# Two attention steps to a turn, query tiles in halves, and an adjacency that is transposed before it is scaled

## The chip, the cores and the metric

The kernel runs on one core of a Trainium2 chip. The metric is the device time of one execution in microseconds (us), as the median of some runs. Every run counted here was in the fast state (its granted clock and its time agree with the fastest of the same kernel), so fast runs are compared with fast runs. A profile names the engines PE (TensorE), PEld (its weight loads), DVE (VectorE), ACT (ScalarE), POOL (GpSimd) and SP. L473 is line 473 of that kernel's source. The changed kernel's lines stand 15 or 16 higher in the attention part than the same lines before.

## The reference

Sixteen batches of 1024 nodes with 256 features. Layer 0 aggregates with a normalized adjacency and runs two linear layers with batch norms; layer 1 is graph-weighted attention with four heads of 64. Each layer is followed by a residual and a layer norm.

```python
# layer 0
A_norm = A + jnp.eye(n)
deg = jnp.sum(A_norm, axis=0) + jnp.sum(A_norm, axis=1) - jnp.diagonal(A_norm)
dinv = jax.lax.rsqrt(deg)
A_hat = A_norm * dinv[:, None] * dinv[None, :]
agg = jnp.einsum('nm,bmd->bnd', A_hat, features)
# ... relu(batchnorm(agg @ W1.T + b1)), then batchnorm(h @ W2.T + b2)
# layer 1 (cut): Wg = adj * a symmetric gate from the column means of x
g = jax.nn.relu(jnp.einsum('bcn,bnm->bcm', fea, Wg) * para)      # the queries
k, v = ...                                                       # x @ kv_w
attn = jax.nn.softmax(jnp.einsum('bhnd,bhmd->bhnm', q, k) * scale, axis=-1)
out = jnp.einsum('bhnm,bhmd->bhnd', attn, v)
```

## The kernel before

The preamble sums the columns of A with one-column matmuls (`pd`), scales the rows of A, transposes A (`pat`) and scales again while the transposes are evicted.

```python
pd = ps.tile([P, FB], F32, tag="a", name="pd")
for j in range(NT):
    for i in range(NT):
        nc.tensor.matmul(pd[:, j : j + 1], A[i][:, ts(j, P)], ones, start=(i == 0), stop=(i == NT - 1))
# ... deg, dinv, A[i] scaled by dinv on VectorE, then transposes (pat) evicted with the second scale
```

Attention runs in 16 steps a batch. A step is one scores product `s` (with its exponentials on ACT), one product `o` of exponentials and values, and between them "fillers": work that prepares the next batch or finishes the last one. All fillers share three PSUM banks, the pool `ps_t`.

```python
ps_s = pool("ps_s", 2, space=PSUM)      # scores, two tiles of two banks
ps_o = pool("ps_o", 1, space=PSUM)
ps_t = pool("ps_t", 3, space=PSUM)      # every filler: pf, px, py, pg, pk, pv, pc, pd

def x1_t(b, j):                          # filler: px, evicted by ACT
    p = ps_t.tile([P, FB], F32, tag="t", name="px")
    for c in range(CT):
        nc.tensor.transpose(p[:, ts(c, P)], x1s[b, j][:, ts(c, P)], ident)
    nc.scalar.copy(x1Ts[b][:, :, ts(j, P)], p[:, :C].rearrange("p (c n) -> p c n", c=CT))

def finish_a(b, i):                      # filler: pf, read by two VectorE instructions
    p = ps_t.tile([P, FB], F32, tag="t", name="pf")
    # ... three transposes into p
    nc.vector.reciprocal(rd, p[...])
    nc.vector.tensor_mul(r, p[...], rd)  # cut: views and broadcast; p is free after this
    nc.vector.tensor_add(r, r, x1s.pop((b, i)))
    # ... statistics of r, nm on GpSimd

for g in range(...):                     # the plan: at[g] holds the fillers of step g
    scores(g + 1); exps(g + 1); sums(g)
    for f, a in at.get(g, []):
        f(*a)
    attend(g)
```

The other fillers are `ln1_a` (py, read by VectorE), `graph` (pg, eight 512-column matmuls into one bank), `keys` (pk), `values` (pv), `crow` (pc, row sums `cs` made into a row) and `dens` (pd, denominators).

Of the kernel before, what the change touches and what calls it, by code (L numbers as in the profile page):

```python
# [9 lines left out]
F32 = mybir.dt.float32  # L10
AF = mybir.ActivationFunctionType
OP = mybir.AluOpType
AX = mybir.AxisListType
# [3 lines left out]
P = 128  # L17
# [5 lines left out]
def gnn_norm_attention_kernel(  # L23
# [16 lines left out]
    nc = tc.nc  # L40
    B, N, C = x.shape
# [4 lines left out]
    FB = 512  # L46
# [31 lines left out]
    yT_all = dram.tile([B, P, CT, N], F32, name="yT")  # L78
    yT_dram = [yT_all[b] for b in range(B)]

    LDP = 3
    s2 = const.tile([P, CT], F32, name="s2")
    t2 = const.tile([P, CT], F32, name="t2")

# [1 line left out]
    with ExitStack() as l0:  # L86
# [29 lines left out]
        with ExitStack() as ph1:  # L116
# [21 lines left out]
            w2n = xp.tile([P, CT, H], F32, tag="w2n", bufs=1, name="w2n")  # L138
            nc.sync.dma_start(w2n, W2.rearrange("(c p) d -> p c d", p=P))
            load_x(0)  # L140
            b1t, g1t, be1t = (load_vec(v, HT, n) for v, n in ((b1, "b1t"), (g1, "g1t"), (be1, "be1t")))
            b2t, g2t, be2t = (load_vec(v, CT, n) for v, n in ((b2, "b2t"), (g2, "g2t"), (be2, "be2t")))
            load_x(1)

            deg = w0.tile([P, NT], F32, name="deg")
            diag = w0.tile([P, NT], F32, name="diag")
            scr = w0.tile([P, P], F32, name="scr")
            for i in range(NT):
                blk = A[i][:, ts(i, P)]
                nc.vector.tensor_add(blk, blk, ident)  # L150
                nc.vector.tensor_reduce(deg[:, i : i + 1], A[i], AX.X, OP.add)
                nc.vector.scalar_tensor_tensor(
                    scr, blk, 1.0, ident, op0=OP.mult, op1=OP.mult, accum_out=diag[:, i : i + 1]
                )

            for c in range(HT):
                p = ps.tile([P, FB], F32, tag="a", name="pw1")
# [6 lines left out]
                    nc.tensor.transpose(p[:, ts(k, P)], w2n[:, c, ts(k, P)], ident)  # L164
                nc.scalar.copy(W2T[:, :, ts(c, P)], p.rearrange("p (k f) -> p k f", k=HT))

            pd = ps.tile([P, FB], F32, tag="a", name="pd")
            for j in range(NT):
                for i in range(NT):
                    nc.tensor.matmul(  # L170
                        pd[:, j : j + 1], A[i][:, ts(j, P)], ones, start=(i == 0), stop=(i == NT - 1)
                    )
            nc.vector.tensor_add(deg, deg, pd[:, :NT])
            nc.vector.tensor_sub(deg, deg, diag)
            dinv = w0.tile([P, NT], F32, name="dinv")
            rsqrt(dinv, deg, 0.0)

            AhT = ahp.tile([P, NT, N], F32, name="AhT")
            for i in range(NT):
                nc.vector.tensor_scalar_mul(A[i], A[i], dinv[:, i : i + 1])  # L180
            for j in range(NT):
                for h in range(NH):
                    p = ps.tile([P, FB], F32, tag="a", name="pat")
                    for k in range(FB // P):
                        i = h * (FB // P) + k
                        nc.tensor.transpose(p[:, ts(k, P)], A[i][:, ts(j, P)], ident)
                    if h % 2:
                        nc.vector.tensor_scalar_mul(AhT[:, j, ts(h, FB)], p, dinv[:, j : j + 1])
                    else:
                        nc.scalar.mul(AhT[:, j, ts(h, FB)], p, dinv[:, j : j + 1])  # L190


            def aggregate(b):
                aggT.append(aggp.tile([P, CT, N], F32, tag="agg", name=f"agg{b}"))
                for c in range(CT):
                    for h in range(NH):
                        p = ps.tile([P, FB], F32, tag="a", name="pa")
                        for k in range(NT):
                            nc.tensor.matmul(  # L199
                                p,  # L200
                                xts[b][:, k, ts(c, P)],
                                AhT[:, k, ts(h, FB)],
                                start=(k == 0),
                                stop=(k == NT - 1),
                            )
                        nc.scalar.copy(aggT[b][:, c, ts(h, FB)], p)  # L206
                load_x(b + 2)
# [113 lines left out]

    def ln_stats(sm, r, name):

        st = sm.tile([P, 6], F32, tag="st", name=f"st_{name}")
        nc.vector.bn_stats(st, r)
        mv = sm.tile([P, 2], F32, tag="mv", name=f"mv_{name}")
        nc.vector.bn_aggr(mv, st)  # L327
        rs = sm.tile([P, 1], F32, tag="rs", name=f"rs_{name}")
        rsqrt(rs, mv[:, 1:2], EPS)
        return mv, rs  # L330
# [4 lines left out]
    def fast():  # L335
      with ExitStack() as fx:
        pool = lambda name, bufs, **k: fx.enter_context(tc.tile_pool(name=name, bufs=bufs, **k))
        x1p = pool("x1p", 21)
        x1Tp = pool("x1Tp", 1)
        crp = pool("crp", 1)  # L340
        wgp = pool("wgp", NT)
        kp = pool("kp", 2 * CT)
        qp = pool("qp", CT + 1)
        vp = pool("vp", 2)
        ep = pool("ep", 5)
        accp = pool("accp", 3)
        otp = pool("otp", 3)
        sm = pool("sm", 6)
        rp = pool("rp", 4)
# [13 lines left out]

        def begin(b):
            x1Ts[b] = x1Tp.tile([P, CT, N], F32, tag="x1T", name=f"x1T_{b}")
            css[b] = sm.tile([P, NT], F32, tag="cs", name=f"cs_{b}")

        def ln1_a(b, j):
            p = ps_t.tile([P, FB], F32, tag="t", name="py")
# [25 lines left out]
        def crow(b):  # L395

            nc.vector.tensor_scalar_mul(css[b], css[b], 1.0 / C)
            hcs[b] = sm.tile([P, NT], F32, tag="hcs", name=f"hcs_{b}")
            nc.vector.tensor_scalar_mul(hcs[b], css[b], 0.5)
            crows[b] = crp.tile([P, N], F32, tag="crow", name=f"crow_{b}")  # L400
            for h in range(NH):
                p = ps_t.tile([P, FB], F32, tag="t", name="pc")
                for k in range(FB // P):
                    j = h * (FB // P) + k
                    nc.tensor.transpose(p[:, ts(k, P)], css[b][:, j : j + 1].to_broadcast([P, P]), ident)  # L405
                nc.scalar.copy(crows[b][:, ts(h, FB)], p)
# [44 lines left out]
        def graph(b, m):  # L451

            h, c, k = m // (CT * NT), m // NT % CT, m % NT
            if k == 0:
                pg[b] = ps_t.tile([P, FB], F32, tag="t", name="pg")
                if h == 0:
                    qTs[b, c] = qp.tile([P, N], F32, tag="qT", name=f"qT_{b}_{c}")
            nc.tensor.matmul(  # L458
                pg[b], x1s[b, k][:, ts(c, P)], wgs[b, k][:, ts(h, FB)], start=(k == 0), stop=(k == NT - 1)
            )  # L460
            if k == NT - 1:
                qs = qTs[b, c][:, ts(h, FB)]
                nc.vector.tensor_mul(qs, pg[b], para_sb[:, c, ts(h, FB)])
                nc.vector.tensor_scalar(qs, qs, 0.0, scale, op0=OP.max, op1=OP.mult)

# [6 lines left out]
        def scores(g):  # L472
            b, hf, pair, cp = step(g)  # L473
            for a in range(2):
                cb = 2 * cp + a
                t = ps_s.tile([P, 2, FB], F32, tag="s", name=f"s{g}_{a}")
                for h in range(2):
                    nc.tensor.matmul(  # L478
                        t[:, h, :],
                        kTs[b, pair][h * HD : (h + 1) * HD, ts(cb, P)],  # L480
                        qTs[b, pair][h * HD : (h + 1) * HD, ts(hf, FB)],
                        start=True,
                        stop=True,
                    )
# [99 lines left out]
            nc.vector.tensor_add(badi[0], bad[:, 0:1], bad[:, 1:2])  # L584


        NS = NT // 2 * NP * NH
        at = {}

        def put(w, s, f, *a):  # L590
            at.setdefault(w * NS + s, []).append((f, a))

        for b in range(B):

            put(b - 2, 4, begin, b)
            for j in range(NT):
                if b > 0 or j >= LDP:
                    put(b - 2, 3 + j, load, b, j)
                put(b - 2, 4 + j, bn2, b, j)
                put(b - 2, 5 + j, ln1_a, b, j)  # L600
                put(b - 2, 7 + j, ln1_b, b, j)
                put(b - 2, 8 + j, x1_t, b, j)
            put(b - 2, 7 + NT, crow, b)
            for i in range(NT):
                put(b - 2, 8 + NT + i, wg_a, b, i)
                put(b - 2, 8 + NT + i, wg_b, b, i)

            n = 0
            kv = [(keys, (b, c, h)) for c in range(CT) for h in range(NH)]
            kv += [(values, (b, j)) for j in range(0, NT, 2)]  # L610
            for n, (f, a) in enumerate(kv):
                put(b - 1, n * 5 // len(kv), f, *a)
            ng = CT * NH * NT
            for m in range(ng):
                put(b - 1, 6 + m * 10 // ng, graph, b, m)

            for i in range(NT):
                hf = i // (FB // P)
                s = (hf + 1) * (NS // NH)
                if i % (FB // P) == 0:  # L620
                    put(b, s, dens, b, hf)
                put(b, s + 1 + i % (FB // P), finish_a, b, i)
                put(b, s + 2 + i % (FB // P) + (b == B - 1 and hf == NH - 1), finish_b, b, i)
        put(B - 1, NS // NH, range_so_far)
        put(B - 1, NS + FB // P, range_all)

        nsteps = B * NS
        for g in range(min(at), max(max(at), nsteps - 1) + 1):
            if 0 <= g + 1 < nsteps:
                scores(g + 1)  # L630
                exps(g + 1)
            if 0 <= g < nsteps:
                sums(g)
            for f, a in at.get(g, []):
                f(*a)
            if 0 <= g < nsteps:
                attend(g)
        return nc.values_load(
            badi[0][0:1, 0:1],
            min_val=0,  # L640
# [156 lines left out]
```

## Time and profile before

| | us |
|---|---|
| time, median of 3 runs | 2816.97 |
| first aggregation matmul (pa) | 62.4 |
| first scores | 1012.0 |
| from one batch's first scores to the next, 13 times | 114.92 |
| last scores end to the end of the span | 20.6 |

The prediction shows the page and the chain. One more view is needed here: what TensorE waited for in one steady batch (the one after seven others). The columns are engine, tile and line that waited, what released it, us in total, times, and the longest.

```profile
PE pc L405 <- DVE cs L397: 1.2, 1, 1.2
```

That is the whole answer: in 114.92 us TensorE waits once. Whatever makes a batch shorter must shorten TensorE's own stream.

### The profile page before, as it was taken

How to read it: one execution, taken by the hardware profiler on the slowest of the kernel's cores; microseconds unless marked ns; L12 is line 12 of the kernel's file. 1: busy time of each engine (PE TensorE's matmuls, PEld its weight loads, DVE VectorE, ACT ScalarE, POOL GpSimd, SP SyncE). 2: the span in 40 equal slices, each digit the busy share in tenths (PEclk: the TensorE clock that was granted, in tenths of full speed). 3: DMA queues.
4: the chain of work that ended last, by engine and by line, in shares of the span. 5: the costliest groups of instructions: out<-in, count | busy, mean ns of one | idle time of the engine just before them, and what ended most of it. 6: DMA issues, size and time to landing. Idle time of an engine off the chain costs nothing.

```text
span 2816.4 us, 26243 instructions
## 1 busy us (share of the span) xinstructions
PE 2750.9 (98%) x9426; PEld 1174.2 (42%) x9426; DVE 1352.6 (48%) x2364; ACT 1295.2 (46%) x1871; POOL 498.2 (18%) x660
## 2 busy tenths in 40 slices
PE   7999999999999899999999999999999999999998
PEld 6444444444444443434434434344343443434432
DVE  3011110111312456657666576575766756657556
ACT  1111111111555654646646556465564664655634
POOL 0000000000000113223122231232322313223113
PEclk9999999999999899999999999999999999999999
DMA  3121221130384200101001010010100100101000
GB/s 105 60 75 60 90 84 65 76 119 0 134 306 142 81 29 27 34 12 43 25 23 34 16 41 27 19 40 16 36 30 16 42 23 27 34 14 42 10 8 24
DMA packets 109993, 147.02 MB, mean 52 GB/s; under 512 B 10272, under 2 KB 92704, under 8 KB 103712
## 3 DMA queue, kind: packets, MB, share of 16 engines
q1 hardware_dynamic: 109856, 145.27, 15.0%
q8 instruction: 77, 1.26, 0.2%
q14 instruction: 60, 0.49, 0.1%
HBM read 86.52 MB, written 58.72 MB: 52 GB/s over the span
## 4 chain that ended last, share of the span: by engine, by line
PE 96%; DVE 2%; DMA 0%; ACT 0%; issue 0%; POOL 0%; SPq 0%; DVEq 0%; POOLq 0%; ACTq 0%
PE s L478 17%; PE o L508 17%; PE pg L458 16%; PE pa L199 16%; PE po L288 8%; PE ph L212 8%; PE pk L431 4%; PE pv L442 4%; PE pf L538 2%; PE pd L527 1%; PE py L371 1%; PE pd L170 1%; PE px L392 1%; PE pc L405 1%; PE pf L539 0%; DMA w1n<-in_L_gnn_W_dram 0%
## 5 line engine op out<-in xcount | busy, mean ns | idle before, releaser
L490 ACT ACTIVATE e<-s 128x1024 f32<-128x1024 f32 x512 | 496.4, 1022 | 409.2 <-PE s L478 408.7
L478 PE MATMUL s<-qT,kT 64*128 64x512 f32 x2048 | 508.8, 615 | 0.0
L508 PE MATMUL o<-e,v 128*64 128x512 f32 x2048 | 495.7, 605 | 0.0
L499 DVE TENSOR_TENSOR acc<-acc,e 128x1024 f32<-128x1024 f32 x384 | 466.9, 1216 | 41.5 <-ACT e L490 27.5
L458 PE MATMUL pg<-wg,x 128*128 128x512 f32 x1024 | 475.4, 602 | 1.5 <-DVE wg L423 1.3
L199 PE MATMUL pa<-AhT,x 128*128 128x512 f32 x1024 | 441.9, 592 | 0.0
L231 DVE BATCH_NORM_STATS2 st<-ph 128x6 f32<-128x512 f32 x128 | 89.4, 698 | 567.3 <-ACT hT L230 567.3
L478 PEld LDWEIGHTS s<-qT,kT 64*128 64x128 f32 x2048 | 176.2, 186 | 327.0 <-issue 244.8
L199 PEld LDWEIGHTS pa<-AhT,x 128*128 128x128 f32 x1024 | 194.5, 190 | 244.4 <-issue 244.2
L458 PEld LDWEIGHTS pg<-wg,x 128*128 128x128 f32 x1024 | 181.6, 190 | 240.5 <-issue 213.0
L423 DVE SCALAR_TENSOR_TENSOR wg<-wg,adj_sb 128x1024 f32<-128x1024 f32 x128 | 156.8, 1225 | 171.7 <-ACT wg L419 169.5
L206 ACT COPY agg<-pa 128x512 f32<-128x512 f32 x64 | 37.5, 586 | 402.3 <-PE pa L199 402.3
L212 PE MATMUL ph<-agg,W1T 128*128 128x512 f32 x512 | 222.2, 592 | 0.0
L508 PEld LDWEIGHTS o<-e,v 128*64 128x64 f32 x2048 | 124.2, 136 | 225.5 <-issue 212.6
L66 POOL TENSOR_SCALAR rs_z<-mv_z 128x1 f32<-128x1 f32 x128 | 52.2, 408 | 900.3 <-DVE mv_z L327 884.4
L66 POOL TENSOR_SCALAR rs_a<-mv_a 128x1 f32<-128x1 f32 x128 | 124.8, 975 | 435.8 <-DVE mv_a L327 435.7
L288 PE MATMUL po<-hL,W2T 128*128 128x512 f32 x384 | 165.0, 592 | 0.0
L68 POOL TENSOR_TENSOR rs_a<-rs_a,mhalf 128x1 f32<-128x1 f32 x128 | 157.9, 1234 | 10.7
L66 POOL TENSOR_SCALAR rs_bn<-mv_bn 128x1 f32<-128x1 f32 x6 | 1.3, 222 | 894.7 <-DVE mv_bn L104 894.7
L393 ACT COPY x1T<-px 128x256 f32<-128x256 f32 x128 | 47.7, 372 | 239.9 <-PE px L392 239.9
L212 PEld LDWEIGHTS ph<-agg,W1T 128*128 128x128 f32 x512 | 97.3, 190 | 122.5 <-issue 122.2
L230 ACT COPY hT<-ph 128x512 f32<-128x512 f32 x128 | 75.0, 586 | 144.7 <-PE ph L212 144.7
(101 smaller groups left out, 2540.7 us busy)
## 6 DMA issues: line engine op xcount, KB each, us to landing
h<-hT SPq DMA_DIRECT2D x24, 1024.0 KB, 3.8
hL<-h SPq DMA_DIRECT2D x24, 1024.0 KB, 6.4
x<-in_x_dram SPq DMA_DIRECT2D x16, 1024.0 KB, 5.4
yT<-y SPq DMA_DIRECT2D x32, 512.0 KB, 3.6
yt<-yT SPq DMA_DIRECT2D x128, 128.0 KB, 2.5
xr<-in_x_dram SPq DMA_DIRECT2D x128, 128.0 KB, 2.3
out_dram<-r SPq DMA_DIRECT2D x128, 128.0 KB, 1.7
A<-in_adj_dram SPq DMA_DIRECT2D x4, 1024.0 KB, 8.3
```

The lines of the kernel that those rows point to most:

```text
L66: nc.gpsimd.tensor_scalar(dst, src, add, None, op0=OP.add)
L68: nc.gpsimd.tensor_tensor(dst, src, mhalf[:, :n], OP.pow)
L199: nc.tensor.matmul(p, xts[b][:, k, ts(c, P)], AhT[:, k, ts(h, FB)], start=(k == 0), stop=(k == NT - 1),)
L212: nc.tensor.matmul(p, W1T[:, k, ts(f, P)], aggT[b][:, k, ts(h, FB)], start=(k == 0), stop=(k == CT - 1),)
L288: nc.tensor.matmul(po[c], W2T[:, k, ts(c, P)], hT[u][:, k, :], start=(k == 0), stop=(k == HT - 1))
L423: nc.vector.scalar_tensor_tensor(t, t, 1.0, adj_sb[:, i, :], op0=OP.add, op1=OP.mult)
L431: nc.tensor.matmul(p, kvw[:, k, ts(c, P)], x1Ts[b][:, k, ts(h, FB)], start=(k == 0), stop=(k == CT - 1))
L458: nc.tensor.matmul(pg[b], x1s[b, k][:, ts(c, P)], wgs[b, k][:, ts(h, FB)], start=(k == 0), stop=(k == NT - 1))
L478: nc.tensor.matmul(t[:, h, :], kTs[b, pair][h * HD : (h + 1) * HD, ts(cb, P)], qTs[b, pair][h * HD : (h + 1) * HD, ts(hf, FB)], start=True ...
L490: nc.scalar.activation(E[g, a], S.pop((g, a)), AF.Exp)
L499: nc.vector.tensor_add(ACC[b, hf, pair], ACC[b, hf, pair], E[g, a])
L508: nc.tensor.matmul(O[b, hf, pair][h * HD : (h + 1) * HD, :], vs[b][:, cb, pair * P + h * HD : pair * P + (h + 1) * HD], E[g, a][:, h, :], ...
```

## The change

The intent is to save two things: the column-sum matmuls ahead of the first useful work, and the changes of tile shape on TensorE. Two steps now make a turn, with one run of fillers in it, and every filler gets a new place in one of eight turns a batch. The query tiles are cut into halves so that they can be freed sooner. The pools are resized to match (E 5 to 6, acc 3 to 2, x1 21 to 22). `ps_t` keeps its three banks.

```diff
 preamble (cut)
-            pd = ps.tile([P, FB], F32, tag="a", name="pd")
-            ... NT * NT one-column matmuls, A scaled, transposes evicted with a scale
+            for h in range(NH):
+                ...
+                        nc.tensor.transpose(p[:, ts(k, P)], A[i][:, ts(j, P)], ident)   # raw A
+                    ... evicted with accum_out=col[:, h, j : j + 1], on VectorE or ACT
+            ... deg and dinv, then both scales in one VectorE instruction a row block
 plan (cut)
+        WG = (3, 3, 1, 1)
+        KV = (3, 3, 2)
+        QG = (6, 6, 6, 7, 7)
+                put(b - 2, j // 2 + 2, ln1_a, b, j)        # two py in a turn
+                put(b - 2, j // 2 + 4, x1_t, b, j)         # two px in a turn
+                    put(b, t + 1 + k // 2, finish_a, ...)  # two pf in a turn
+            put(b - 2, NC - 1, crow, b)
 loop (cut)
-        for g in ...: scores(g + 1); exps(g + 1); sums(g); fillers; attend(g)
+        rank = {dens: 0, finish_a: 1, finish_b: 2, x1_t: 3, ln1_a: 4, ln1_b: 5}
+        for t in ...:
+            g = 2 * t
+            now = sorted(at.get(t, []), key=lambda fa: rank.get(fa[0], 9))
+            scores(g + 2); exps(g + 2); dens of now; sums(g)
+            the other fillers of now; sums(g + 1)
+            scores(g + 3); exps(g + 3)
+            attend(g); attend(g + 1)
```

Note the sort: in each turn all pf come first, then px, then py, and only then the long products pg, pk and pv.

> **What bounds the kernel now.** I read the page's engine shares, then the chain that ended last, then the timeline of TensorE and of the engines it works with, in three stretches.
>
> ```profile
> span 2816.4 us, 26243 instructions
> PE 2750.9 (98%) x9426; PEld 1174.2 (42%) x9426; DVE 1352.6 (48%) x2364; ACT 1295.2 (46%) x1871; POOL 498.2 (18%) x660
> ...
> PE 96%; DVE 2%; DMA 0%; ACT 0%; issue 0%; POOL 0%; SPq 0%; DVEq 0%; POOLq 0%; ACTq 0%
> ```
>
> TensorE (PE) carries 96% of the chain; VectorE (DVE) and ScalarE (ACT) have half their time free. A change helps only where it shortens TensorE's own stream or removes its waits. The long pieces of the chain of waits, in order of time, show the preamble:
>
> ```profile
> 3.01 12.11 DMA w1n<-in_L_gnn_W_dram
> 18.90 27.11 PE pd L170 x128
> 48.18 5.40 DVE A L180 x8
> 53.63 8.90 PE pat L186 x57
> 62.53 54.94 PE pa L199 x128
> ```
>
> Useful matmuls start at 62.4 us. Before them stand 27 us of one-column matmuls (column sums of A), a rescaling, the transposes. After that the chain has 429 ns per matmul instruction (54.94/128), the full rate for 512 columns. Marks by stage, from first starts of groups in the timeline: aggregation 62.4, second linear layer 723, its end 945, first scores 1012.0, last scores end 2795.8. In attention a batch of 16 steps takes 114.92 us, the same thirteen times over. One step on TensorE (start, length):
>
> ```profile
> 1656.34 2.74 PE L458 MATMUL pg<-wg,x 128*128 128x512 f32 x6
> 1658.91 0.38 PE L392 MATMUL px<-ident,x 128*128 128x128 f32 x2
> 1659.13 0.38 PE L371 MATMUL py<-ident,yt 128*128 128x128 f32 x2
> 1659.44 1.94 PE L508 MATMUL o<-e,v 128*64 128x512 f32 x8
> 1661.31 1.99 PE L478 MATMUL s<-qT,kT 64*128 64x512 f32 x8
> 1663.23 0.44 PE L538 MATMUL pf<-ident,ot 128*128 128x128 f32 x2
> ```
>
> Eight instructions of o or s run as four pairs, so 4 x 0.429 = 1.72 us at full rate; from start to start o takes 1.87 and s 1.92. From raw starts: leaving any group for one of another tile shape costs 0.09 us, and the second start in the new shape comes 0.10 late (s, pg, pk) or 0.05 late (o, transposes). So TensorE never waits here, except once per batch (1.2 us, pc for DVE's cs), but pays about 0.5 us per step in three shape switches. And the chain that frees a pf buffer, on VectorE:
>
> ```profile
> 1656.54 0.18 DVE L541 RECIPROCAL RD<-pf 128x4 f32<-128x4 f32 x1 [0.72 <-PE pf L539]
> 1656.75 0.42 DVE L543 TENSOR_TENSOR r<-pf,RD 128x256 f32<-128x256 f32 x1
> 1657.21 0.43 DVE L548 TENSOR_TENSOR r<-r,x 128x256 f32<-128x256 f32 x1
> 1657.67 0.43 DVE L325 BATCH_NORM_STATS2 st_z<-r 128x6 f32<-128x256 f32 x1
> 1658.13 0.18 DVE L327 BATCH_NORM_AGGREGATE mv_z<-st_z 128x2 f32<-128x6 f32 x1
> 1658.23 0.45 DVE L379 SCALAR_TENSOR_TENSOR x<-x,mv_a,rs_a 128x256 f32<-128x256 f32 x1
> ```
>
> The pf buffer is free when L543 ends, 0.9 us after the last pf transpose starts; a second finish behind it on VectorE begins 1.69 us later. Today one pf stands in a step and nothing needs its buffer soon.
>
> **What the Trainium skill says.** "TensorEngine Tiling (Array Packing)", Key Properties: changing the tiling mode drains TensorE. The trace agrees: the 0.14 to 0.20 us per switch above. "PSUM — Partial Sum Buffer" gives 8 banks of 2 KiB per partition: scores (2 x 2 banks), o (1) and the ps_t pool (3) use all, so ps_t can't grow. "Trainium Kernel Development and Optimization", Best Practices: consistent bubbles can mean that PSUM ran out; the kernel before shows none, and I expect them now. "TensorE: Matmul & The Clock Gate", Part 1: the clock is halved until TensorE has been busy for a window. The trace agrees: transposes start every 213 ns until 58.7 us and every 109 after.
>
> **The change, part by part.**
>
> *Preamble.* A is transposed raw, column sums come from accumulating evictions, and both scales are applied afterwards, so the 27 us of pd go, and the transposes no longer wait for them. New path: A lands from 5.7 us (first VectorE work) to about 13 (4 MB at the 415 GB/s of that window). 32 cold transposes x 0.213 = 6.8 us per half. VectorE is slower: per half four diagonals (0.29 + 0.36), two row sums of 1.22 and four evictions of about 0.8, some 8.5 us with waits; both halves end near 24.7. Degree sums 0.6, the power on POOL 1.7 (L68 dinv took 1.66), four cold transposes 0.9, first scaling 0.75: pa starts at 29. Scaling one row block (0.7) is faster than its two matmuls (0.86), so it stays ahead. Cold clock for the first matmuls: 1 to 3 us lost. Net -31 us.
>
> *Shape switches.* A turn is s, fillers, s, o, o instead of twice s, fillers, o. The second o follows the first without a switch: -0.15 us per turn, 1.2 per batch. There are 8 runs of fillers per batch instead of 16, each 0.15 to 0.20 for entering and leaving: -1.4. Scores still enter twice. Sum -2.6 us per batch. Scores, o and filler matmuls themselves are the same number.
>
> *Buffers.* The plan now puts two finishes, two px and two py in one turn, all transposes first. In the new program's order and its waits, with three ps_t banks (often one held by pg), I find for a steady batch, turns 0 to 7, time from the start of the turn's first scores (1.92 long; exps done at 3.1, as the exponentials of the step above start 1.17 after their scores and take 1.94; pf at 1.92 and 2.31, its reciprocal 0.59 later as above; a px copy on ACT starts 0.42 after px, as 1658.91 to 1659.33 shows, and takes 0.37):
> - Turn 5: px waits for the first pf's buffer (L543 ends 3.15); the second px for ACT's copy of the first (4.07); py for the next copy (4.9); the second py for the second pf's buffer, free at 4.84 (2.51 + 1.69 + 0.64). pg resumes at 5.36 instead of 3.51: 1.85 us lost.
> - Turn 6: px at 3.2, its copy is behind two 0.6 us finish activations on ACT (exps till 3.1, so copied at 4.75); pg at 5.0 instead of 3.1: 1.9.
> - Turn 4: px and py wait for the dt copy and px copies: pg at 4.84 instead of 3.85: 1.0.
> - Turn 2: pv waits for the second pf's buffer, 4.9 instead of 3.08: 1.8.
> - Turn 7: pc directly follows pg rather than px, so its wait for cs (qT 0.69 + 0.43, cs 0.17) grows by 0.2.
> - Turns 0, 1, 3: pk or pg separate the reuses; ACT (11 to 13 us of work in turns of 13.5) and VectorE (at most 13.2) keep up; no loss.
> Sum +6.75. Query halves only free qT earlier (5 half buffers are enough); nobody waited for qT, so worth 0.
>
> Net per steady batch -2.6 + 6.75 = +4.2 us. Fourteen windows have the full plan, the first without turn 2: 14 x 4.2 - 1.8 = +57. The next to last has no px or py and gains 2.4, the last gains 1. Start-up: without attention to cover it, ACT's wg before the kT copies and pairs of layer norms cost a little, +2 to the first scores. At the end four o groups instead of two follow the last scores: +3.6.
>
> Sum: -31 + 57 - 3.4 + 2 + 3.6 = +28, so 2845 us.
>
> **Rivals.**
> *(a) The waits don't happen* or hide: then -2.6 x 16 - 31 + 3 = -70, about 2748, faster by 2.5%. For it: VectorE and ACT average half idle, and every engine passes its per-turn sum. Against: the waits stand in the program, matmuls run in order, and each latency is one that the trace shows at its shortest, with the waiting engine idle.
> *(b) More waits than counted*: VectorE in turns 1 and 2 (13.2 of 13.5 us, then both finishes) falls behind, so finishes begin late, or exps(g+3), behind all ACT fillers and needing E buffers that only o(g) frees, delays the next scores. Each 1 us per turn in two turns is 28 us: near 2875, slower by 2%. For it: the sums on VectorE come last in the turn; against: two attends (3.6 us) of slack.
> *(c) The preamble alone matters*: if attention comes out even, about 2790. That needs the losses to halve.
>
> **Range and chances.** The preamble is uncertain by 4 us, start-up and end by 4, switches (s to o has no record yet) by 6, the buffer waits by 1 us per batch, or 14. Together 18 for one deviation; with (a) and (b) as tails: 2810 to 2875. Faster by over 2% (under 2760.6) needs (a): 0.08. Slower by over 2% (over 2873.3): 0.12. Within: 0.80.
>
> **What would show it.** First pa at 29 to 32 us instead of 62.4. In attention, a period near 119 us per batch; idle before px, py, pg and pv on TensorE, released by L543's successor on VectorE and by ACT's x1T copies, about 6.5 us per batch, in four of eight turns; TensorE busy near 94% in attention. o's second group starts 0.43 us after the last pair of the first, not 0.52. Wrong if the period is under 115 (waits hidden), if scores themselves wait for exps (then (b)), or if pa starts after 36 us.

## The result, and the profile after

The changed kernel is correct and takes 2846.47 us (median of 4 runs, 2846.23 to 2846.97), against 2816.83 for the kernel before in the same rounds. The ratio is 1.0106, 95% interval 1.0089 to 1.0124: the same within 2%, and 1% slower. Ratios here and below are the mean time of one kernel's fast runs over the mean of the other's fast runs of the same rounds, so they are not quite the ratios of the medians quoted.

The page of the changed kernel:

```profile
span 2844.6 us, 26117 instructions
...
PE 2713.6 (95%) x9306; PEld 1157.5 (41%) x9306; DVE 1349.9 (47%) x2377; ACT 1289.3 (45%) x1887; POOL 321.0 (11%) x660
```

TensorE was busy for 2750.9 us of 2816.4 before and is for 2713.6 of 2844.6 now: it works 37 us less and stands idle 65 us more. (The page's chain of waits was followed back only over the last few us of this kernel, so it says nothing here.)

The preamble is in TensorE's timeline (start, length, line, tile, and in brackets the idle time before it and what ended that):

```profile
9.65 6.58 PE L170 MATMUL pat<-ident,A 128*128 128x128 f32 x50
...
23.32 1.09 PE L188 MATMUL pdr<-ident,dinv 128*128 128x128 f32 x8 [1.85 <-POOL dinv L68]
24.95 5.37 PE L215 MATMUL pa<-AhT,x 128*128 128x512 f32 x8 [0.54 <-issue]
```

The aggregation starts at 24.95 instead of 62.37. The first eight matmuls take 5.37 us where full speed takes 3.4, as the clock is halved from 25.2 to 28.7. The first scores come at 976.51 instead of 1012.04, so 35.5 us earlier.

Attention gives all of it back. The period is 119.19 us instead of 114.92. These are TensorE's waits in one steady batch, the whole answer, in the columns of the one line before:

```profile
PE pc L421 <- DVE cs L413: 1.4, 1, 1.4
PE pv L458 <- DVE r L558: 1.4, 1, 1.4
PE px L408 <- ACT x1T L409: 1.2, 2, 0.7
PE px L408 <- DVE r L558: 1.0, 2, 0.5
PE py L387 <- ACT x1T L409: 0.7, 2, 0.5
PE px L408 <- ACT dt L544: 0.4, 1, 0.4
PE py L387 <- PE py L387: 0.2, 1, 0.2
```

Every tile that waits is a filler, and every releaser (`r L558`, `x1T`, `dt`) but two is the instruction that reads another filler's bank last. The two are `cs`, which pc needs as data, and py itself. Turn 5 of this batch shows how, first on TensorE:

```profile
1893.96 0.38 PE L553 MATMUL pf<-ident,ot 128*128 128x128 f32 x2
1894.18 0.27 PE L554 MATMUL pf<-ident,dt 128*128 128x128 f32 x1
1894.95 0.41 PE L408 MATMUL px<-ident,x 128*128 128x128 f32 x2 [0.50 <-DVE r L558]
1895.83 0.44 PE L408 MATMUL px<-ident,x 128*128 128x128 f32 x2 [0.46 <-ACT x1T L409]
1896.72 0.66 PE L387 MATMUL py<-ident,yt 128*128 128x128 f32 x4 [0.46 <-ACT x1T L409]
```

then on VectorE and on ACT at the same time:

```profile
1894.38 0.42 DVE L558 TENSOR_TENSOR r<-pf,RD 128x256 f32<-128x256 f32 x1
...
1896.04 0.42 DVE L558 TENSOR_TENSOR r<-pf,RD 128x256 f32<-128x256 f32 x1
```

```profile
1895.40 0.37 ACT L409 COPY x1T<-px 128x256 f32<-128x256 f32 x1 [0.62 <-PE px L408]
1896.30 0.37 ACT L409 COPY x1T<-px 128x256 f32<-128x256 f32 x1 [0.53 <-PE px L408]
```

The turn starts at 1891.66. The first px starts when the first pf's product ends (1894.38 + 0.42 = 1894.80), the second px when the copy of the first has ended (1895.77), py when the next copy has (1896.67). ACT waited for px and TensorE for ACT: both were idle by turns, TensorE for about 0.5 us at each hand-over. Before, a step held at most one pf, one px and one py: in the prediction's excerpt six 512-column products stand between pf and px, px and py follow each other without a wait, and the next px comes a step later.

I measured the waits turn by turn from TensorE's start-to-start times, counting what exceeds the interval of an undisturbed pair (109 ns for a transpose, 216 for pv, 429 for the 512-column products). This counts from start to start, so it comes out a little larger than the idle times of the view above.

| turn | length before | length after | of it waits | where |
|---|---|---|---|---|
| 7 | 17.45 | 16.50 | 1.58 | pc |
| 0, 1, 3 | 42.17 | 40.32 | 0 | |
| 2 | 11.79 | 14.15 | 1.93 | second py, pv |
| 4 | 14.55 | 15.64 | 0.88 | second px, second py |
| 5 | 15.41 | 16.31 | 1.92 | px, second px, py |
| 6 | 13.55 | 16.28 | 1.53 | px, second px |

Fillers moved between turns, so single lengths before and after do not compare; their sums do (114.92 and 119.20), and the waits of a turn do with its own order. In the kernel before the only entry is 1.36 for pc.

One thing had not been foreseen. Two of the thirteen steady periods are 120.88 and 120.86 us long, and the record of the clock shows it halved for 3.4 us in turn 5 of each. These are stretches of the changed kernel with the busy time of each engine (TensorE's first) and the granted clock as the third value from the end. The first two rows are such a place, the last two the same place one batch earlier:

```profile
1653.40:1656.80 3.40, 1.98 (x13) 1.19 (x12) 2.50 (x8) 2.05 (x4) 0.75 (x2) 1.00 0.00 0
1656.80:1660.20 3.40, 3.40 (x8) 1.84 (x8) 3.19 (x12) 0.00 (x0) 2.45 (x9) 0.50 0.03 5
1534.20:1537.60 3.40, 1.98 (x13) 1.18 (x12) 2.49 (x8) 2.06 (x4) 0.75 (x2) 1.00 0.00 0
1537.60:1541.00 3.40, 3.40 (x12) 1.73 (x13) 3.19 (x12) 0.00 (x0) 2.44 (x9) 1.00 0.00 0
```

Both stretches hold the same matmuls and the same three waits, yet only one was followed by half clock, at a cost of 1.7 us. All changes of the clock in this trace lie on multiples of 3.4133 us from each other (the two halvings are 210 multiples apart). On that grid the first stretch fills one window, and the one a batch earlier lies across two, as the period of 119.19 is 34.92 windows and the waits slide over the grid. That this decides when the clock is halved is likely, but not shown. How long TensorE was busy in a window does not decide it by itself: the two windows before the halvings hold 1.99 us of work, but seven windows in turn 2 of the same trace hold 1.81 us (1731.91 to 1735.32 is one), and none of them was followed by half clock.

### The profile page after: what moved, and what is told of

Same layout as the page of the kernel before. It is cut to its first block, busy times and chain, and to the rows that moved or that the text cites. A ratio compares the mean times of both kernels' runs of the same rounds, so it can differ in the third digit from the quotient of the medians.

```text
span 2844.6 us, 26117 instructions
## 1 busy us (share of the span) xinstructions
PE 2713.6 (95%) x9306; PEld 1157.5 (41%) x9306; DVE 1349.9 (47%) x2377; ACT 1289.3 (45%) x1887; POOL 321.0 (11%) x660
## 5 line engine op out<-in xcount | busy, mean ns | idle before, releaser
L523 PE MATMUL o<-e,v 128*64 128x512 f32 x2048 | 467.7, 598 | 0.0
L473 PE MATMUL pg<-wg,x 128*128 128x512 f32 x1024 | 455.6, 595 | 0.0
L473 PEld LDWEIGHTS pg<-wg,x 128*128 128x128 f32 x1024 | 189.5, 191 | 210.6 <-issue 203.9
L523 PEld LDWEIGHTS o<-e,v 128*64 128x64 f32 x2048 | 135.6, 136 | 316.4 <-issue 315.6
L511 DVE TENSOR_TENSOR acc<-e,e 128x1024 f32<-128x1024 f32 x64 | 78.2, 1222 | 206.1 <-PE pd L542 206.1
L439 DVE SCALAR_TENSOR_TENSOR wg<-wg,adj_sb 128x1024 f32<-128x1024 f32 x128 | 155.2, 1221 | 38.6 <-ACT wg L435 35.1
L66 POOL TENSOR_SCALAR rs_z<-mv_z 128x1 f32<-128x1 f32 x128 | 37.5, 293 | 1197.7 <-DVE RD L556 1168.6
L478 DVE TENSOR_TENSOR qT<-pg,para_sb 128x512 f32<-128x512 f32 x64 | 44.2, 690 | 199.2 <-PE pg L473 198.9
L458 PE MATMUL pv<-kvw,x1T 128*128 128x256 f32 x512 | 116.8, 381 | 17.8 <-DVE r L558 17.8
L308 DVE BATCH_NORM_STATS2 st<-po 128x6 f32<-128x512 f32 x64 | 44.8, 700 | 169.3 <-PE po L304 169.3
```

The source lines that it names most:

```text
L439: nc.vector.scalar_tensor_tensor(t, t, 1.0, adj_sb[:, i, :], op0=OP.add, op1=OP.mult)
L458: nc.tensor.matmul(p[:, ts(a, C)], x1Ts[b][:, k, ts(j + a, P)], kvw[:, k, C:], start=(k == 0), stop=(k == CT - 1),)
L473: nc.tensor.matmul(pg[b], x1s[b, k][:, ts(c, P)], wgs[b, k][:, ts(h, FB)], start=(k == 0), stop=(k == NT - 1))
L511: nc.vector.tensor_add(ACC[b, hf, pair], E[g, 0], E[g, 1])
L523: nc.tensor.matmul(O[b, hf, pair][h * HD : (h + 1) * HD, :], vs[b][:, cb, pair * P + h * HD : pair * P + (h + 1) * HD], E[g, a][:, h, :], ...
```

## The experiments

The theory: waits for `ps_t` banks cost about 6.5 us a batch, because the sorted order puts the short transposes together, and the rest of the change does what it should. The rivals: (b) VectorE or ACT fall behind over the turn, (c) the attention plan comes out even. Nine kernels ran, all correct. Medians of 4 or 5 runs; 2816.9, 2817.6 and 2814.9 for the kernel before in the three batches of runs.

### Parts alone

The first has the preamble alone, the second everything but it.

```diff
# kernel before
-   preamble of the kernel before (from the first load of x to the first hidden layer)
+   preamble of the changed kernel
# kernel after: the same exchange the other way
```

> The kernel before with only the raw-transpose preamble, the attention plan untouched. If the parts add up (my theory), the 35.7 us by which the second layer started earlier in the changed kernel come out in full at the end: about 2781 us, 1.3% faster than before; first pa near 25 us, attention period 114.9 us as before. If the earlier start only moves a wait (the start of attention then waits for ACT or the loads), it is nearer 2795 to 2815.

Measured: 2781.82 us, ratio 0.988 (0.9864 to 0.9897). The first pa is at 24.56, the period 114.92.

> The changed kernel with the old preamble put back. If the parts add up: 2846.5 + 35.7 = about 2882 us, 2.3% slower than before, period 119.2 us per batch as in the changed kernel. Rival (c), that the attention plan comes out even and something else in the changed kernel costs the time, would give about 2817.

Measured: 2879.30 us, ratio 1.0226 (1.0209 to 1.0243), period 119.19. The parts add up: -35.1 and +62.4 make +27.3, and the whole change made +29.6. The difference of 2.3 us is explained in part: in the second kernel pa came at 59.3 rather than at 62.4 (full clock from 55.7 rather than 58.7), which saved it 3.1 us, and a third half-clock stretch cost it 1.7. Rival (c) falls: the preamble is worth 35 us and the new plan costs 62.

The query halves alone, on the kernel before:

```diff
-        qp = pool("qp", CT + 1)                 # whole tiles [P, N]
+        qp = pool("qp", 2 * CT + 1)             # halves [P, FB], one for each (b, c, h)
```

> The kernel before with only the query tiles cut into halves. Nothing waited for a query tile, so my theory expects no change: within 2 us of the kernel before (2816.8), period 114.9. If whole query tiles held the graph product back, it is faster by several us per batch.

Measured: 2816.26 us, ratio 0.9999 (0.9984 to 1.0014), period 114.92. They cost and save nothing.

### The same fillers in another order

This is the test that separates the theory from rival (b). The work of a turn stays what it is; only its order changes (on VectorE and ACT too, whose instructions move with the fillers).

```diff
# kernel after
+        def spread(t, now):                 # in turns 2, 4, 5 and 6
+            ... light = finish_a, x1_t, ln1_a;  heavy = graph, keys, values
+            for i in range(max(len(light), len(heavy))):
+                out += light[i : i + 1] + heavy[i : i + 1]
+            # turn 2: pf, finish_b, pv, pf, pv, py, py
             now = sorted(...)
+            now = spread(t, now)
```

> The changed kernel with the same work in the same turns, but in turns 2, 4, 5 and 6 the transposes alternate with graph or value matmuls instead of standing all first; no buffer is added. Buffer theory: the waits in those turns (6.26 us per batch) vanish, the period falls from 119.2 to about 112.9 us, and the two stretches of half clock in turn 5 vanish with them: about 2755 us, 2.2% faster than before and 3.2% faster than the changed kernel. Rival (b), VectorE and ACT falling behind over the whole turn: the order inside a turn does not matter, so it stays near 2846, or the waits move to scores.

Measured: 2750.80 us, ratio 0.977 (0.9754 to 0.9786), so faster than the kernel before by 2.3%. The period is 112.47, and no clock drop occurs in attention. Turns 2, 4, 5 and 6 take 12.12, 14.60, 14.26 and 14.68 us, with no wait left; the others are unchanged. Of the seven lines of waits in a steady batch this one remains:

```profile
PE pc L421 <- DVE cs L413: 1.4, 1, 1.4
```

Turn 5 in the changed kernel and in this one, as stretches with each engine's busy time:

```profile
1891.66:1907.97 16.31, 14.88 (x61) 6.08 (x59) 10.43 (x25) 4.62 (x6) 3.74 (x10) 1.00 0.00 1
```

```profile
1842.17:1856.43 14.26, 14.26 (x60) 5.88 (x58) 10.44 (x25) 4.63 (x6) 3.94 (x10) 1.00 0.00 1
```

VectorE has 10.43 and 10.44 us of work and ACT 4.62 and 4.63: the same, and the turn is 2.05 us shorter with TensorE busy throughout. Rival (b) falls for this kernel. The order cost the time, not the amount of work of any engine; three banks are enough in the right order. (No run has another number of banks. That the order acts through the banks is read from the releasers in the waits above.)

Next, pc in turn 7 moved in between the graph products (the two px of that turn, which had no wait, are spread as well):

```diff
-        SPREAD, CROW = (2, 4, 5, 6), False
+        SPREAD, CROW = (2, 4, 5, 6, 7), True     # crow counts as light in turn 7
```

> As the spread one, and in turn 7 the row sum of the graph (pc) stands between the graph matmuls rather than just behind the product whose buffer it needs. Buffer theory: the 1.58 us wait for pc goes too, period about 111.3 us, about 2732 us, 3% faster than before. If pc waits for VectorE's column sums rather than for a bank, it stays and the time is that of the spread one.

Measured: 2733.25 us, ratio 0.9707 (0.969 to 0.9723), period 111.19; turn 7 is 15.21 instead of 16.50, and the wait for pc is 0.27 instead of 1.58. The time alone doesn't tell bank from data, as `cs` is computed on VectorE in the same filler and moves with pc. The traces do: in the changed kernel cs starts at 1695.56, right behind the two VectorE instructions for the last graph product (1694.49 to 1695.65), and pc at 1695.87; here cs starts at 1751.66, 0.75 us into the turn, with those two far behind it. So pc waited for its data, and the expectation was wrong on that point, though right on the time. It is the fastest kernel of this study, with a variant below that ties with it, and 2.9% faster than before.

It also gives the gain of fewer shape changes. Without the waits for pc, a batch takes 111.19 - 0.27 = 110.92 here and 114.92 - 1.36 = 113.56 in the kernel before, with the same matmuls: 2.64 us less. (The order of the fillers differs as well; the last run below varies the number of shape changes almost alone.)

### One reader moved

Here both finishes' reads of PSUM go ahead on VectorE.

```diff
# kernel after: finish_a ends behind the product that reads pf; the rest becomes finish_c
-        rank = {dens: 0, finish_a: 1, finish_b: 2, ...
+        rank = {dens: 0, finish_a: 1, finish_c: 1.5, finish_b: 2, ...
```

> The changed kernel with one thing moved on VectorE: the reciprocal and the product that read pf stand ahead of the rest of both finishes, so the second pf's bank is free about 1 us sooner. Buffer theory: only turn 2 (pv for the second pf) shrinks, by about 1.0 us of its 1.5; turn 5 and 6 wait on ACT's copies as well and keep nearly all: about 1 us per batch, 2833 us. Rival (b), total work of VectorE: the work is the same, so no change, 2846.

Measured: 2823.14 us, ratio 1.0022 (1.0007 to 1.0037), period 117.53: 23 us less than the changed kernel, where I had expected 13. Rival (b), as a matter of VectorE's total work, is again refuted, as that work is the same. But the turns share it differently: turn 2 gains only 0.50, turn 5 gains 0.57 and turn 6 0.59. In turn 5:

```profile
1884.74 0.96 PE L408 MATMUL px<-ident,x 128*128 128x128 f32 x4 [0.50 <-DVE RD L556]
1885.61 0.99 PE L387 MATMUL py<-ident,yt 128*128 128x128 f32 x4
```

Both px now run together: the second no longer waits for ACT's copy of the first. The likely reason is that it takes the second pf's bank: VectorE's product on that ends at 1885.13, 3.68 us into the turn, and in the changed kernel at 1896.46, 4.80 into it. In turn 2, pv has a new wait behind the one taken away, for the reader of py (0.4 us). Banks go to whoever comes next, so a bank freed earlier in one place changes who waits in another. A sum of single waits, each taken as it stood, is not a forecast of what removing one of them gives.

### The end and the number of shape changes

In the changed kernel four o groups follow the last scores, two before. This variant of the fastest kernel was meant to put the attends of the last turn ahead of its second scores. Its edit moves only one of them: in the trace three o groups (x24) follow the last scores, and not the two that were expected.

```diff
+            if g + 4 == nsteps:
+                attend(live.pop(0))
             if ahead:
                 scores(g + 3)
```

> The spread kernel with pc moved, and in the very last turn the attends stand ahead of the second scores so that two instead of four o groups follow the last scores. Expected 3 to 4 us below the one without it, about 2728 us, 3.1% faster than before.

Measured: 2733.33 us, ratio 0.9707 (0.9694 to 0.972): no gain. TensorE's timeline of this kernel and then VectorE's:

```profile
2712.09 1.05 PE L542 MATMUL pd<-acc,ones 128*32 128x512 f32 x4
2714.17 1.05 PE L542 MATMUL pd<-acc,ones 128*32 128x512 f32 x4 [1.03 <-DVE acc L514]
```

```profile
2706.28 7.84 DVE L514 TENSOR_TENSOR acc<-acc,e 128x1024 f32<-128x1024 f32 x6
```

The second pd waits for six additions on VectorE, 7.84 us in one burst behind the finishes of the previous half. The burst starts at 2706.28 here and at 2706.56 in the kernel without this edit, and the first pd at 2712.09 and 2712.22: the edit swaps an o group with a scores group and takes no work from TensorE ahead of pd, so it could not gain what was expected of it. That VectorE sets the time of the second pd is read from its wait (1.03 us here, 1.19 without the edit); the edit adds only that the order moved nothing.

Two last kernels vary the number of shape changes from the four a turn of the fastest one: three (both scores, both attends, then fillers) and five (the first attend ahead of the fillers).

```diff
# three
-            scores(g+2), exps; sums(g); fillers; sums(g+1); scores(g+3), exps; attends
+            scores(g+2), exps; scores(g+3), exps; sums(g), sums(g+1); attends; fillers (dens first)
# five
+            attend(g) directly behind sums(g)
```

> The spread kernel with pc moved, its turn reordered to both scores, both attends, fillers: three changes of tile shape a turn instead of four, with no work added or removed. A change of shape costs 0.14 (into o or a transpose) to 0.19 us (into scores) by start-to-start times, so 0.19 us a turn, 1.5 a batch: period 109.7 instead of 111.2 us, about 2710 us in all, 3.8% faster than before. If shape changes are not what a turn saves, it stays at 2733; if the second exponentials, which now need the E buffers that the first attend frees, hold TensorE up, it is slower than that.

Measured: 2957.04 us, ratio 1.0507 (1.049 to 1.0525): a miss by 247 us. TensorE's waits and one of ACT's in a steady batch of this kernel (126.16 us):

```profile
PE s L493 <- ACT e L505: 7.7, 8, 3.8
PE px L408 <- ACT dt L544: 2.6, 1, 2.6
```

```profile
ACT e L505 <- DVE acc L511: 14.2, 2, 7.1
```

I had overlooked two buffers. The two score tiles in PSUM hold one step, so a second scores product right behind the first has to wait for its exponentials, about 0.42 us in most turns (start to start). And I had put the sums ahead of the denominators. With two acc buffers the first sum of a new half then waits for the denominators of the last, the exponentials wait for the E buffers that this sum reads (7.1 us), and the next scores wait for the exponentials (3.8). The clock adds to this: it was halved in 25 stretches of this kernel's attention, 92 us together, two of them in the batch shown. Here rival (b)'s chain is real: the changed kernel avoids it by keeping the two scores apart and the denominators first. What three shape changes would save by themselves stays untested.

> The counterpart: the first attend of each turn stands ahead of the fillers, so five changes of shape a turn as in the kernel before (per two steps six there). Expected 0.14 us a turn more, 1.15 a batch: period 112.3 us, about 2750 us. If the pairing of two attends is not what saved the time, it stays at 2733.

Measured: 2750.67 us, ratio 0.9772 (0.9756 to 0.9788), period 112.08. Every turn but turn 7 is longer by 0.15 us, for one more shape change; in turn 7 the last wait for pc (0.27 us) vanished as well, so a batch costs 0.89 us more and not 1.15. The cost of a shape change holds.

## Why the prediction was right

The time was predicted at 2845 and measured at 2846.5, and the mechanism is the predicted one. Step by step, for the profiled runs:

| term | predicted | measured |
|---|---|---|
| preamble, and start-up of attention | -31 and +2 | -35.5 together |
| shape changes a batch | -2.6 | -2.64 (fastest kernel, waits taken off) |
| waits of turns 2, 4, 5, 6, each | 1.8, 1.0, 1.85, 1.9 | 2.03, 1.04, 2.05, 1.60 |
| their sum | 6.55 | 6.72 (period less that of the spread one) |
| pc | +0.2 | +0.22 |
| net of a steady batch | +4.2 | +4.27 |
| first window | +2.4 | +0.8 |
| 13 steady windows | +54.6 | +55.5, and +3.5 in the longer ones (half clock) |
| last two windows | -3.4 | -1.6 |
| end | +3.6 | +5.5 |
| sum | +28 | +28.2 |

*Preamble.* The largest miss of a single term. I had both halves of A transposed by 24.7 us and pa at 29; the evictions were done at 20.9. VectorE set the pace, as I had it, and the first half took it 8.3 us, where I had 8.5. Of the 3.8 us between my 24.7 and the 20.9, 2.0 are a slip in my sum: two halves of 8.5 us from 5.7 on end at 22.7. And the second half took 6.85 (from 14.04 to 20.89), because its evictions followed each other every 0.61 us rather than 0.8 and it waited for no transpose, with the clock full from 11.6. The loss to the cold clock at the start of pa did come (1.7 us, in my range of 1 to 3). Attention's start-up cost nothing: py first started 35.7 us earlier than before, and the first scores 35.5. The sign "first pa at 29 to 32" did not come true.

*Buffers.* The turns were right, and the sum of the waits by 3%. The order of releases that I gave for turn 5 is the one in the trace: px at 3.29 us from the turn's start (3.15 predicted for the product's end, 3.14 measured), the second px at 4.17, py at 5.06, pg at 5.56 (5.36 predicted). In turn 6 I was 0.3 us high: px started at 3.29 (3.2 predicted) and its copy stood behind two finish activations on ACT, as predicted, but those took 1.09 us together and the copy ended at 4.35, where I had 4.75. That turns 0, 1 and 3 lose nothing held too.

*Half clock.* Missing from the prediction: 3.4 us over two batches. They come with the waits as this order packs them, since the spread kernel has none in attention.

*End.* Four o groups instead of two follow the last scores, 7.09 - 3.65 = 3.4 us, as predicted. But they are moved and not added: in the first batch's window 14 o groups start instead of 15, in the last 15 instead of 16. I had taken them off nowhere, so the terms for the first window, the last two and the end belong together: +2.6 predicted, +4.7 measured. Another 2.2 us at the end are the denominators' wait for VectorE's additions, which I had not looked at; by the trace this sets the end.

*Rivals.* (a), no waits, would have been right only with another order: the kernels with the fillers spread came to 2750.8 and 2733.3. (b) didn't happen, but is one careless reordering away. (c) failed at both ends: the preamble alone gave 2781.8, and attention did not come out even.

The errors of -6.5 us in the preamble and its start, and of about +6.5 in all that follows, cancel. So the total fits better than its parts do, and the small difference of 1.5 us is partly luck. (The 18 us of the range are a little more than its parts 4, 4, 6 and 14 give as the root of the sum of squares, 16.)

## What to carry to other kernels

When short producers share a few PSUM banks, low load of the readers is no safeguard: the distance between two uses of a bank in the order of TensorE can decide. Here a long product between every two short ones hid the readers' latency, with the same three banks. A gain in the stream of the bounding engine (here 2.6 us a batch) is only real if the same edit doesn't draw dependent uses together. Work out the bank releases from the instruction order and from latencies in the old trace, turn by turn; that gave the loss to within 3%, where average engine loads of a half would have promised a gain.

## What the Trainium skill lacked or had wrong

- "TensorE: Matmul & The Clock Gate", Part 1: its table has the clock halved after "≥1 idle window (~3.4µs)", and it says that the window is free-running. The grid agrees: all changes of the clock in the changed kernel lie on multiples of 3.4133 us. But the window need not be idle, as the same part says further on of short idles between groups of matmuls: two windows with 1.99 us of TensorE work in 3.41 (by the trace's modelled matmul ends) and no single wait over 0.66 us were followed by half clock. What the page lacks is how much work keeps the clock up; these runs don't show it either, as windows with 1.81 us did not lose it.
- The same page, Part 4: it says that the full clock doesn't engage for transpose mode. Here a stream of nothing but transposes brought it: their start-to-start time went from 213 ns to 109 ns at 11.6 us, during the 18th. The trace doesn't show whether these matmuls with an identity run in that mode.
- "TensorEngine Tiling (Array Packing)", Key Properties: it says that a mode change drains TensorE, but not what that costs. In the kernel before it is 0.09 us on leaving a shape plus 0.05 (into o or transposes) or 0.10 (into scores) inside the next group; one more such change a turn, in the last run above, made the turn 0.15 us longer.
- No page read for this case says how the time that a PSUM bank stays taken follows from the reader's queue: a pf bank was free 0.95 us after the start of its last transpose for the first pf of turn 5, and 2.28 us for the second, whose reads stood behind the first one's statistics on VectorE.
